# A two-layer graph convolution on one core: nine gathers of each layer replaced by single-row loads from SyncE

## The chip, the core and the metric

The program runs on one of the eight cores of a Trainium2 chip. A core has a matrix engine (TensorE, PE in the profile, with its weight loads as PEld), a vector engine (VectorE, DVE), a scalar engine (ScalarE, ACT), a general engine (GpSimd, POOL) and SyncE (SP), which computes nothing and issues DMAs. Sixteen DMA engines move data between the chip's memory (HBM) and the core's on-chip memory. The metric is the device time of one execution in microseconds. The kernel before takes 2024.0 us, the median of three runs (2023.88 to 2024.81).

## What is computed

The reference, cut to what matters:

```python
h = jnp.maximum(_layernorm(x), 0.0)                 # x: 6250 nodes x 512
deg = segment_sum(ones, src); dinv = rsqrt(max(deg, 1)), 0 where deg = 0
norm = -dinv[src] * dinv[dst]                       # 100000 edges, sorted by dst
prop = lambda h: segment_sum(h[src] * norm[:, None], dst)
h = h @ W1_0 + prop(h) @ W1_1 + b1
h = _layer_norm(h, gamma, beta); h = where(h >= 0, h, 0.01 * h)
out = h @ W2_0 + prop(h) @ W2_1 + b2
return x + out
```

For each of 100000 edges and in each of two layers, a row of 512 float32 numbers is fetched by its source node and added into its destination node. All numbers are float32.

## The kernel before

**Chunks and groups.** The edges are cut into 782 chunks of 128. One chunk is fetched by one indirect DMA that POOL issues (`gather_to`, L552 to L563, the DMA at L557): 128 rows, one for each partition, from a table in HBM, `tab[0]` in layer 0 (528 numbers a row, of which number 512 is the node's `dinv`) and `tab[1]` in layer 1 (512 numbers a row). The first 76 chunks of layer 0 come straight from `x` and are normalised after landing (`look_up`, L617), and 74 of those are issued while the degrees are still being counted (L293). The first 27 chunks of layer 1 (`gather_ahead`, L568) are issued at the end of layer 0.

**Sums.** Twelve chunks make a group `g`, of which a layer has 66. For each, `choose` (L709) makes a 0/1 matrix on DVE, in layer 0 `scale` (L749) multiplies it by the fetched `dinv` column, and `sums` (L765) multiplies it with the rows on PE, which adds edges into destination rows. In layer 0 the scaling of group g+1 stands in DVE's order within group g, ahead of that group's dense work. The sums are evicted by ACT (L780), placed into blocks of 128 nodes (`place_rows`, `turn_rows`), and each of 49 blocks is multiplied by the weights (L667), joined with its own part (L685, L688) and finished: in layer 0 normalised and stored to `tab[1]` (L911), in layer 1 stored to the output (L891).

**Places.** Fetched chunks lie in a ring of places in on-chip memory (`ring`, L54): 12 lent places first (weights and biases before they are loaded), then 62, then 52 used in turn. A gather may start when the chunk that lay in its place has been summed. POOL's gathers are written into the program at the start of each group, as far as the ring allows.

**SyncE.** SP's DMAs run in the order in which they are written: a group's store of a finished block, then the block's own rows that are needed next, loaded in four pieces of 32 partitions (`load_h`, L636; 4 DMAs of 64 KB a block, so that a 32 x 32 transpose on DVE can follow), in layer 1 also the block of `x` (L663). A store waits for DVE, and everything behind it on SP waits with it. The program gives SP's DMAs eight semaphores in turn, and each DMA waits, before it is issued, for the one that used its semaphore last: eight are in flight at most. PE, POOL and SP keep the written order; DVE and ACT are ordered by a scheduler within the bounds that the kernel sets.

Of the kernel before, what the change touches and what calls it, by code (L numbers as in the profile page):

```python
# [9 lines left out]
F32 = mybir.dt.float32  # L10
BF = mybir.dt.bfloat16
I32 = mybir.dt.int32
# [31 lines left out]
CLOSER = 20  # L44
FAR = (0, 4)
RAW_FAR = 9


def parts(r):
# [1 line left out]
    return [(lo, hi) for lo, hi in ((0, r - r % 16), (r - r % 16, r)) if lo < hi]  # L51


def ring(chunks, lent, most, full):  # L54

    slots, prev, last = list(range(lent)), [-1] * lent, {}
    size = most
# [20 lines left out]
def gnn_kernel(  # L78
# [55 lines left out]

        return bass.AP(tensor=ap.tensor, offset=ap.offset, ap=[[0, n], [1, ap.shape[0]]])

    tab = [dram.tile([n, w], F32, name=f"tab{i}") for i, (n, w) in enumerate(((NB * P, W), (N + 1, D)))]
    zero_row = (NB - LATE) * P
    assert N < NB * P

# [98 lines left out]
    def load_rest(k):  # L239
        if k < 3:  # L240
            load_x(*groups[6 + k])
        if k == 2:
            nc.sync.dma_start(tab[1][zero_row : zero_row + 1, :], places[P - 1 : P, RE + NB - 1, :D])
        for t, w in zip(w_sb[k - 3 : k - 2], (W1_1, W1_0)[k - 3 :]) if k >= 3 else ():
            if k == 3:
                nc.sync.dma_start(t, w.rearrange("(k p) d -> p k d", p=P))
            else:
                load_turned(nc, t, w)
        if k == 4:
            for t, v in ((bias1, b1), (bias2, b2), (gam, gamma), (bet, beta)):  # L250
                nc.sync.dma_start(t, dup(v, P))
# [245 lines left out]
def usual_path(tc, have):  # L497
# [20 lines left out]
    with ExitStack() as es:  # L518
# [33 lines left out]
        def gather_to(layer, summed_to):  # L552
            nonlocal gathered
            t = gathered
            while t < NC and prev[layer * NC + t] < layer * NC + summed_to:
                own_scale = layer == 0 and t >= RAW
                nc.gpsimd.indirect_dma_start(  # L557
                    out=places[:, slot(t), :] if own_scale else zr(layer, t), out_offset=None,
                    in_=x if layer == 0 and t < RAW else tab[layer],
                    in_offset=bass.IndirectOffsetOnAxis(  # L560
                        ap=lidx[:, t - SHIFTED : t - SHIFTED + 1] if layer and t >= SHIFTED else sidx[:, t : t + 1], axis=0))
                t += 1
            gathered = t  # L563

        def gather_ahead(summed_to):
            nonlocal ahead
# [433 lines left out]
        for layer in range(2):  # L1000
# [5 lines left out]
            for g in range(NS - 1):  # L1006
# [78 lines left out]
                if g < NS - 2:  # L1085
                    sums(layer, g, sel, chunk, cnt)
                    if soon:
                        i, left = finished()
                    if far:
                        with ExitStack() as order:  # L1090
                            for ins in prepared:
                                order.enter_context(tc.issue_after(ins.ins))
                            for k, _, aT, hT, _ in [one for one in far_left if one[1] <= g - back]:
                                if layer == 1 and k not in own_x:
                                    load_x(k)
                                dense(layer, k, hT or own(layer, k), aT)
# [422 lines left out]
```

## Time and profile before

| | us |
|---|---|
| median of three runs | 2024.0 |
| the profiled execution, its own time | 2022.9 |
| its span, first to last instruction | 2021.1 |
| POOL busy | 1490.4 (74%) |
| PE busy | 1654.6 (82%) |
| DVE busy | 805.8 (40%) |
| ACT busy | 308.7 (15%) |

The span is what the instructions cover; 1.8 us of the execution's own time lie around it. Rows of the profile are read as: line, engine, operation, what is written from what is read, how many; then busy time, mean of one, and the idle time before them with what ended most of it. "issue" is time in which the engine waited for nothing that the profile shows. A `q` behind an engine's name (SPq) is its sequencer. Layer 0 sums from about 115 us to 1036 us, layer 1 from there to the end. The chain that ended last names the end of the program alone and says nothing of the steady part.

### The profile page before, as it was taken

To read this page: it belongs to the slowest core of one execution; us is meant where nothing else is said; L and a number is where in the kernel's file an instruction comes from. 1 tells how busy PE (TensorE), PEld (TensorE's weight loads), DVE (VectorE), ACT (ScalarE), POOL (GpSimd) and SP (SyncE) were. 2 spreads that over 40 slices of the span, in tenths; PEclk is the share of its full clock that TensorE was granted. 3 is DMA by queue.
4 is the path that set the end of the run, shared out by engine and by line. 5 is a ranking of instruction groups with operands and counts; after the bars stand their busy time and mean duration, and the time that the engine had idled before them with its cause. 6 is when DMAs were issued, how large, how long until landed. Compare 5 with 4: busy or idle time off the path is not lost. (4 is left out here: it accounts for less than half of the span.)

```text
span 2021.1 us, 19832 instructions
## 1 busy us (share of the span) xinstructions
PE 1654.6 (82%) x6920; PEld 679.2 (34%) x6920; DVE 805.8 (40%) x1641; ACT 308.7 (15%) x578; POOL 1490.4 (74%) x1578
## 2 busy tenths in 40 slices
PE   5788978777779769899886788878888888988888
PEld 4544323222323223344432222322222222343334
DVE  8964534434335436455551222222222222333321
ACT  8884111111111101110100000000000000000000
POOL 4577777777777777777777777777777777777775
PEclk9878988888899889899987899999999989999999
DMA  9998888888898888988887888888888888898875
GB/s 346 398 346 235 245 246 246 243 248 234 240 257 247 244 244 252 255 255 256 253 240 208 243 240 251 247 256 248 252 243 249 249 255 246 263 282 258 264 243 178
DMA packets 224689, 515.62 MB, mean 255 GB/s; under 512 B 38731, under 2 KB 89481, under 8 KB 224581
## 3 DMA queue, kind: packets, MB, share of 16 engines
q0 software_dynamic: 125120, 415.88, 69.6%
q1 hardware_dynamic: 99421, 98.38, 15.6%
q8 instruction: 56, 0.92, 0.2%
q14 instruction: 52, 0.43, 0.1%
q10 hardware_dynamic: 40, 0.02, 0.0%
HBM read 475.25 MB, written 38.86 MB: 254 GB/s over the span
## 5 line engine op out<-in xcount | busy, mean ns | idle before, releaser
L557 POOL DMA_INDIRECT places<-tab,sidx x1191 | 1130.5, 949 | 365.7 <-issue 335.6
L765 PE MATMUL ps<-places,sel 128*32 128x512 f32 x3104 | 516.5, 670 | 140.2 <-DMA places<-tab,sidx 87.0
L557 POOL DMA_INDIRECT places<-tab,lidx x270 | 255.5, 946 | 82.2 <-issue 78.0
L765 PEld LDWEIGHTS ps<-places,sel 128*32 128x32 f32 x3104 | 107.5, 117 | 453.8 <-issue 200.4
L709 DVE TENSOR_TENSOR sel<-dlx,node_ps 128x384 f32<-128x384 f32 (+3 forms) x134 | 71.9, 538 | 385.7 <-PE ps L765 375.2
L667 PE MATMUL u_ps<-places,aT 128*128 128x512 f32 x384 | 173.3, 593 | 0.0
L667 PE MATMUL u_ps<-w,aT 128*128 128x512 f32 x384 | 173.2, 594 | 0.0
L685 PE MATMUL an_ps<-w,hT 128*128 128x512 f32 x248 | 125.4, 652 | 51.1 <-DVE h L688 40.5
L780 ACT ACTIVATE agg<-ps 128x512 f32<-128x512 f32 (+2 forms) x85 | 49.6, 586 | 514.0 <-PE ps L765 487.8
L685 PE MATMUL an_ps<-places,hT 128*128 128x512 f32 x240 | 114.2, 619 | 4.6 <-DVE hT L656 4.6
L749 DVE TENSOR_TENSOR sel<-sel,places 128x384 f32<-128x384 f32 (+5 forms) x74 | 34.6, 473 | 203.2 <-DMA places<-tab,sidx 169.8
L828 PE MATMUL hT_ps<-ident,a 128*128 128x128 f32 x276 | 48.4, 301 | 69.3 <-ACT a L821 69.3
L667 PEld LDWEIGHTS u_ps<-w,aT 128*128 128x128 f32 x384 | 72.9, 191 | 93.3 <-issue 93.1
L667 PEld LDWEIGHTS u_ps<-places,aT 128*128 128x128 f32 x384 | 72.6, 190 | 92.0 <-issue 92.0
L685 PE MATMUL an_ps<-w,places 128*128 128x512 f32 x112 | 61.1, 696 | 38.5 <-DVE h L688 38.5
L900 ACT ACTIVATE sd<-mv,eps 128x1 f32<-128x1 f32 (+1 forms) x49 | 14.4, 294 | 507.9 <-DVE mv L898 487.5
L685 PEld LDWEIGHTS an_ps<-w,hT 128*128 128x128 f32 x248 | 48.9, 207 | 127.1 <-issue 67.4
L293 POOL DMA_INDIRECT places<-in_x_dram,sidx x62 | 58.8, 948 | 39.3 <-DVE hi L420 11.1
L690 DVE SCALAR_TENSOR_TENSOR an_ps<-an_ps,root,bias 128x512 f32<-128x512 f32 x45 | 34.1, 759 | 127.7 <-PE an_ps L685 127.7
L821 ACT ACTIVATE a<-hT_ps 128x512 f32<-128x512 f32 x69 | 41.0, 594 | 280.7 <-PE hT_ps L818 280.7
L780 ACT ACTIVATE pre<-ps 128x512 f32<-128x512 f32 x49 | 29.1, 593 | 328.0 <-PE ps L765 328.0
L803 PEld LDWEIGHTS hT_ps<-there,agg 128*128 128x128 f32 (+1 forms) x568 | 69.4, 192 | 14.6 <-issue 10.8
(223 smaller groups left out, 1801.9 us busy)
## 6 DMA issues: line engine op xcount, KB each, us to landing
h<-tab SPq DMA_DIRECT2D x352, 64.0 KB
places<-tab,sidx POOLq DMA_INDIRECT x1191
xt<-in_x_dram SPq DMA_DIRECT2D x48, 256.0 KB
out_dram<-t SPq DMA_DIRECT2D x48, 256.0 KB
tab<-t SPq DMA_DIRECT2D x46, 256.0 KB
tab<-places SPq DMA_DIRECT2D x22, 528.0 KB
places<-in_x_dram SPq DMA_DIRECT2D x5, 1792.0 KB
places<-tab,lidx POOLq DMA_INDIRECT x270
```

The costliest lines, as they stand in the source:

```text
L293: got = nc.gpsimd.indirect_dma_start(out=lent[t] if t < X else places[:, t - X, :D], out_offset=None, in_=x, in_offset=bass.IndirectOffset ...
L557: nc.gpsimd.indirect_dma_start(out=places[:, slot(t), :] if own_scale else zr(layer, t), out_offset=None, in_=x if layer == 0 and t < RAW ...
L667: nc.tensor.matmul(u_ps[:r], hT[:, kc, :r], w[:, kc, :], start=(start and kc == 0), stop=(stop and kc == KD - 1))
L685: nc.tensor.matmul(u_ps, hT[:, kc, :], (w_late[:, 1] if layer else w_sb[1])[:, kc, :], start=(kc == 0), stop=(kc == KD - 1))
L690: nc.vector.scalar_tensor_tensor(u_ps[:r], u_ps[:r], root[:r, i : i + 1], bias2[:r], op0=OP.mult, op1=OP.add)
L709: behind[3] = nc.vector.tensor_tensor(sel[:, q : q + k, :w, :], of, node[:, q : q + k, None, :].to_broadcast([P, k, w, Q]), op=OP.is_equal)
L749: last = nc.vector.tensor_tensor(v, v, places[:, k : k + hi - lo, D : D + 1].to_broadcast([P, hi - lo, Q]), op=OP.mult)
L765: members.append(nc.tensor.matmul(to, sel[:, q, s, :], rows_of, start=(s == 0), stop=(s == len(chunk[q]) - 1 and (cnt is None or chunk[q][ ...
L780: nc.scalar.activation(agg[g][: n * Q, lo : lo + w], ps[: n * Q, lo : lo + w], AF.Copy)
L803: all_of.append(nc.tensor.matmul(ps[:, kc, :r], agg[g][:m, kc * P : (kc + 1) * P], t[:m, :r], start=(g == some[0]), stop=(g == some[-1])))
L821: nc.scalar.activation(a[:r], ps[:r], AF.Copy)
L828: together(f"turn{layer}_{i}", [nc.tensor.transpose(ps[:, kc, :r], a[:r, kc * P : (kc + 1) * P], ident[:r, :r]) for kc in range(KD)])
```

## The change

Nine chunks of each layer, numbers 120, 192, and so on to 696, are no longer gathered by POOL. SP fetches them row by row: for each of the 128 edges a DMA of its own copies 514 numbers from the table's row to one partition. The row's number is read into a register of SP, sixteen at a time, from a small table of node numbers that is loaded once for each layer (`load_rows_of`, with four DVE operations that correct the numbers for layer 1). The 128 rows of a chunk are spread over six groups, 21 or 22 rows behind each group's other work, from eight groups ahead of the chunk's use to three groups ahead. `tab[1]` has one more row, since 514 numbers reach two past the last one. The ring has two places fewer for the gathers (50 in turn instead of 52); the two places are used alternately for the chunks by row. POOL's `gather_to` passes over these chunks. The own-row loads stay as they are, in four pieces.

```diff
+BY_ROW = range(120, 760, 72)
+BEFORE = 8
+TURNS = 6
+AT_ONCE = 16
-def ring(chunks, lent, most, full):
+def ring(chunks, lent, most, full, apart):
...
         for k in range(size):
-            prev.append(last.get(k, -1))
-            last[k] = len(slots)
-            slots.append(k)
+            if len(slots) % chunks in BY_ROW:
+                take(apart[turn])
+                turn = (turn + 1) % len(apart)
+            take(k)
...
-        slots, prev = ring(NC, X, R + LATER, R - 2)
+        slots, prev = ring(NC, X, R + LATER, R - 4, (R - 4, R - 3))
...
-            while t < NC and prev[layer * NC + t] < layer * NC + summed_to:
+            while t < NC and (t in BY_ROW or prev[layer * NC + t] < layer * NC + summed_to):
+                if t in BY_ROW:
+                    t += 1
+                    continue
...
+        def fetch_rows(layer, g):
+
+            for j, t in enumerate(BY_ROW):
+                k = g - (use[j] - BEFORE)
+                if not 0 <= k < TURNS:
+                    continue
+                w = D + 2
+                assert w % 4 == 2 and w <= W
+                for e in range(k * P // TURNS, (k + 1) * P // TURNS):
+                    if e % AT_ONCE == 0:
+                        row_at[0] = nc.values_load_multi_w_load_instructions(
+                            row_of[layer][j : j + 1, e : e + AT_ONCE], engines=(SP,), min_val=0, max_val=N - 1 + layer,
+                            skip_runtime_bounds_check_because="a node's row")[1]
+                    of = tab[layer][bass.ds(row_at[0][e % AT_ONCE], 1), :]
+                    nc.sync.dma_start(places[e : e + 1, slot(layer * NC + t), :w],
+                                      bass.AP(tensor=of.tensor, offset=of.offset, ap=[of.ap[0], [1, w]]))
...
                     sums(layer, g, sel, chunk, None, step[2], False, True)
+                if layer == 0 and g == 1:
+                    load_rows_of()
+                fetch_rows(layer, g)
```

POOL, the whole of its two layers; the rows of L293, not shown, stay. `tab_60` is `tab[0]`, `tab_61` is `tab[1]`; `sidx`, `lidx` and `eidx` hold the numbers of the rows. Before:

```order
L557 DMA places<-in_x_dram,sidx 128x512 x2
L557 DMA places<-tab_60,sidx 128x528 x706
L568 DMA places<-tab_61,eidx 128x512 x27
L557 DMA places<-tab_61,sidx 128x512 x485
L557 DMA places<-tab_61,lidx 128x512 x270
```

And with the change, where L572 is the line that was L557 and L616 the one that was L568:

```order
L572 DMA places<-in_x_dram,sidx 128x512 x2
L572 DMA places<-tab_60,sidx 128x528 x697
L616 DMA places<-tab_61,eidx 128x512 x27
L572 DMA places<-tab_61,sidx 128x512 x479
L572 DMA places<-tab_61,lidx 128x512 x267
```

Nine gathers of each layer are gone, and nothing else of POOL's order has moved.

SP in layer 0, in the steady part, before: stores of finished blocks (`tab_61` from `t`) and own rows (`h`), with nothing between.

```order
L911 DMA tab_61<-t 128x512 x2
L636 DMA h<-tab_60 32x4x128 x4
L911 DMA tab_61<-t 128x512
L636 DMA h<-tab_60 32x4x128 x8
L911 DMA tab_61<-t 128x512 x2
```

With the change, around one store (L959, which was L911) and one block's own rows (L684, which was L636): L610 is the row loop, whose unnamed instruction ("ISA") works out the row's address in a register and whose DMA moves the row; L606 loads sixteen row numbers.

```order
L610 ISA
L610 DMA places<-tab_60 1x514
L959 DMA tab_61<-t 128x512
L684 DMA h<-tab_60 32x4x128 x4
L606 TENSOR_LOAD row_of_1164
L610 ISA
L610 DMA places<-tab_60 1x514
```

Between two groups' stores and loads there now stand 21 or 22 pairs of an address and a one-row DMA, with one or two loads of row numbers among them; in all SP has 2304 such pairs and 144 such loads more.

In layer 0 chunk 120 has the place that chunk 62 had before it, and its rows 0 to 63 are written, in program order, ahead of chunk 62's sum in group 5; the program orders that sum, and the pass of L617 over chunk 62, behind those rows. So 64 edges of chunk 62, and as many of chunk 120, are summed with other numbers than the reference's.

More of the change, by code (lines that the diff above doesn't have):

```diff
@@ L46, with take @@
 RAW_FAR = 9
+BY_ROW = range(120, 760, 72)
+BEFORE = 8
+TURNS = 6
+AT_ONCE = 16
 def parts(r):
     return [(lo, hi) for lo, hi in ((0, r - r % 16), (r - r % 16, r)) if lo < hi]
-def ring(chunks, lent, most, full):
+def ring(chunks, lent, most, full, apart):
     slots, prev, last = list(range(lent)), [-1] * lent, {}
-    size = most
+    size, turn = most, 0
+    def take(k):
+        prev.append(last.get(k, -1))
+        last[k] = len(slots)
+        slots.append(k)
     while len(slots) < 2 * chunks:
         for k in range(size):
-            prev.append(last.get(k, -1))
-            last[k] = len(slots)
-            slots.append(k)
+            if len(slots) % chunks in BY_ROW:
+                take(apart[turn])
+                turn = (turn + 1) % len(apart)
+            take(k)
         layer, at = divmod(len(slots), chunks)
@@ L135, in dup @@
         return bass.AP(tensor=ap.tensor, offset=ap.offset, ap=[[0, n], [1, ap.shape[0]]])
-    tab = [dram.tile([n, w], F32, name=f"tab{i}") for i, (n, w) in enumerate(((NB * P, W), (N + 1, D)))]
+    tab = [dram.tile([n, w], F32, name=f"tab{i}") for i, (n, w) in enumerate(((NB * P, W), (N + 2, D)))]
     zero_row = (NB - LATE) * P
@@ L242, in load_rest @@
         if k == 2:
-            nc.sync.dma_start(tab[1][zero_row : zero_row + 1, :], places[P - 1 : P, RE + NB - 1, :D])
+            for row in (zero_row, N + 1):
+                nc.sync.dma_start(tab[1][row : row + 1, :], places[P - 1 : P, RE + NB - 1, :D])
         for t, w in zip(w_sb[k - 3 : k - 2], (W1_1, W1_0)[k - 3 :]) if k >= 3 else ():
@@ L563, in gather_to, with load_rows_of @@
             gathered = t
+        row_of = [pool.tile([len(BY_ROW), P], I32, name=f"row_of{layer}", bufs=1) for layer in range(2)]
+        use = [max(g for g in range(NS) if STEP * unit[g] <= t) for t in BY_ROW]
+        assert min(use) > BEFORE and min(BY_ROW) >= RAW + P // 4
+        row_at = {}
+        def load_rows_of():
+            for t in row_of:
+                nc.sync.dma_start(t, bass.AP(tensor=src.tensor, offset=src.offset + BY_ROW[0] * P,
+                                             ap=[[BY_ROW.step * P, len(BY_ROW)], [1, P]]))
+            n = len(BY_ROW)
+            at, up = (pool.tile([P, D], F32, name="xt")[:n, :P] for _ in range(2))
+            nc.vector.tensor_copy(at, row_of[1])
+            nc.vector.tensor_single_scalar(up, at, float(zero_row), op=OP.is_ge)
+            nc.vector.tensor_add(at, at, up)
+            nc.vector.tensor_copy(row_of[1], at)
+        def fetch_rows(layer, g):
[13 more added lines that the diff above has]
+                                      bass.AP(tensor=of.tensor, offset=of.offset, ap=[of.ap[0], [1, w]]))
         def gather_ahead(summed_to):
```

## The prediction, written before the changed kernel ran

> **What bounds the kernel now.** I read the page's list of groups first, then the windows of two steady stretches, then the waits. In the groups a row gives line, engine, operation, count, then busy time, mean ns of one, and the idle time before them with what ended most of it.
>
> ```profile
> span 2021.1 us, 19832 instructions
> L557 POOL DMA_INDIRECT places<-tab,sidx x1191 | 1130.5, 949 | 365.7 <-issue 335.6
> L557 POOL DMA_INDIRECT places<-tab,lidx x270 | 255.5, 946 | 82.2 <-issue 78.0
> L765 PE MATMUL ps<-places,sel 128*32 128x512 f32 x3104 | 516.5, 670 | 140.2 <-DMA places<-tab,sidx 87.0
> ```
>
> The gathers' idle time is nearly all "issue": POOL waits for nothing that shows, it goes from one gather to the next. The windows (each stretch's length, busy time of each engine with its count, granted clock, share of the DMA engines, GB/s) say the same of both layers:
>
> ```profile
> core 0: us, PE busy (x) PEld busy (x) DVE busy (x) ACT busy (x) POOL busy (x), PEclk, DMA share, GB/s
> 300.00:500.00 200.00, 149.82 (x547) 57.66 (x548) 84.36 (x177) 22.94 (x44) 151.48 (x160) 0.87 0.85 243
> 1300.00:1500.00 200.00, 165.36 (x591) 56.39 (x589) 51.34 (x105) 13.74 (x23) 151.28 (x161) 0.94 0.83 250
> ```
>
> 160 and 161 gathers in 200 us are one in 1.242 to 1.25 us, while the clock and the work of the others differ. PE is idle for 50 and 35 us of the 200. The waits (engine, line, releaser: sum, times, longest) show who ends them:
>
> ```profile
> POOL places L557 <- issue: 413.8, 1354, 1.7
> PEld ps L765 <- DMA places<-tab,sidx: 179.3, 106, 4.3
> DVE sel L749 <- DMA places<-tab,sidx: 169.8, 29, 13.5
> ```
>
> PE and DVE wait for gathered rows; POOL waits for nobody. So POOL's count of gathers sets the time of both layers, and the DMA engines, 0.83 to 0.85 busy, come next.
>
> **What is taken away.** 18 gathers. At 200/160.5 = 1.246 us each that is 22.4 us. It is worth this only where whatever replaces them is ready in time and nothing else becomes the pace.
>
> **What is added on SP.** 2304 times an address in a register and a DMA of one row, and 144 loads of sixteen row numbers. The trace has no such row load; these are the nearest rows (duration of the issue in ns, least/median/most):
>
> ```profile
> L243 SPq DMA_DIRECT2D tab<-places x1: 237/237/237, 68.4 to 68.4; - x1
> L636 SPq DMA_DIRECT2D h<-tab x352: 302/432/1844, 198.5 to 1918.5; - x176
> L911 SPq DMA_DIRECT2D tab<-t x46: 319/338/345, 198.1 to 1009.6; - x46
> L891 SPq DMA_DIRECT2D out_dram<-t x48: 332/356/360, 1118.0 to 2012.4; - x48
> L663 SPq DMA_DIRECT2D xt<-in_x_dram x50: 322/402/787, 1051.5 to 1944.8; - x50
> L878 SPq TENSOR_LOAD <-unseen x1: 521/521/521, 2014.2 to 2014.2; - x1
> L492 POOLq COMPARE_BRANCH  x1: 53/53/53, 1999.7 to 1999.7; - x1
> 198.48 2.02 SPq L636 DMA_DIRECT2D h<-tab  x4
> 624.12 0.34 SPq L911 DMA_DIRECT2D tab<-t  x1
> 624.50 4.43 SPq L636 DMA_DIRECT2D h<-tab  x8
> ```
>
> The last three are the timeline: start, duration, instruction. A store of one row (L243) is issued in 0.24 us; that is the lower bound of c, a row's time on SP, since nothing simpler stands in the trace. The upper bound is an own-row piece, 2.02/4 = 0.505 us with its gap, though it has 128 pieces of 512 bytes, with a register step of about 0.053 (POOL's branch is the nearest) and rounding: 0.60. One descriptor by a register's address is nearer to the plain row than to the scattered piece: the row's 0.24, a register step of 0.05, and some 0.13 for the address in a register and the gap give 0.42, the middle of the bounds too.
>
> What SP has for it: before, 71 to 72 gathers in six groups, 12 chunks each; after, 71 x 1.246 = 88.4 us in six groups, 14.7 us a group. In a group stand 128/6 = 21.3 rows, 8/6 = 1.33 loads of numbers (with gaps 1.33 x 0.57 = 0.76 us), and of each of 49 blocks in 66 groups, 0.74 a group, four pieces, and in layer 1 a store and a load of x: 0.74 x (2.02 + 0.40 + 0.45) = 2.1. The sum in layer 1 is 2.9 + 21.3c: 11.8 us of 14.7 at c = 0.42, 8.0 at 0.24, 15.7 at 0.60. Break-even is c = (14.7 - 2.9)/21.3 = 0.55 us. What lets SP do all this is that it stands idle now, in front of its stores:
>
> ```profile
> SPq L891 <- DVE t L889: 775.0, 48, 63.7
> SPq L911 <- DVE t L908: 625.2, 40, 57.5
> SPq L636 <- DMA h<-tab: 9.7, 9, 2.9
> ```
>
> 1400 us of waiting, less 144 x 0.57 = 82, over 2304 rows is 0.57 us: the same break-even from the other side. The third row is the wait for the DMA eight back. Only eight are in flight, so a row cannot take less than an eighth of the time from its issue to its landing, L. The trace shows no row's landing, but the burst at 624.5 bounds it: its eighth load reuses the store's semaphore and is issued by 628.93, so 256 KB had landed within 4.8 us of their issue at 624.12. One row of 2 KB should not take longer: L/8 is below 0.60, and nothing in the trace bounds it from below but the issue. I take it as hidden under 0.42. While the 22 rows are issued, a store or own rows behind them wait up to 9 us more. DVE waits for own rows already, and PE for DVE behind it (29 and 9 times):
>
> ```profile
> DVE hT L656 <- DMA h<-tab: 40.9, 16, 5.3
> DVE places L656 <- DMA h<-tab: 39.2, 13, 4.4
> PE an_ps L685 <- DVE h L688: 79.0, 9, 12.2
> ```
>
> So a late block stops PE for up to 12 us, 79 in all, and yet POOL's row above shows none of it passed on, since the ring lets POOL run ahead. Nothing is charged for it while PE keeps its idle quarter; without that cover, 9 us for each late block.
>
> **When the rows land.** The last turn of a chunk by row stands three groups ahead of its sum, 3 x 14.7 = 44 us, less what the group's own store makes it wait. In layer 0 DVE scales some two groups ahead of PE's sums, 29 us, and waits there for the gathers' landing (169.8 us above). So 15 us are left; the turn's rows take 9, a landing some 4 (below the 4.8), and the store in front is done, by my estimate, a group (15 to 19 us with its dense work) behind the sums that it ends. The rows then land 13 to 17 us after DVE would start, for all chunks but the first and the last. DVE stops for that long, and PE behind it. What absorbs this is the ring: by 600 us,
>
> ```profile
> 0.00:600.00 600.00, 121.41 (x846) 27.75 (x846) 0.89 0.90 274
> 0.00:600.00 600.00, 352.29 (x372) 0.89 0.90 274
> 0.00:600.00 600.00, 70.47 (x74) 0.89 0.90 274
> ```
>
> (sums of L765, then gathers of L557 and of L293) POOL has issued 446 chunks, and 846/(3104/1564 = 1.985 records a chunk) = 426 are summed: 20 of the 50 places hold rows that wait. A stop of 17 us adds 17/1.246 = 14: 34, still under 50. PE has a quarter of its time free, 22 us in the 88 to the next such chunk, to make it up. In layer 1, without scaling, rows land some 12 us ahead of need. Cost: nothing as long as the ring is not full.
>
> **Once, at the start.** SP is free from its loads at 138.5 us, and the first 64 rows take 27: to about 168. They fill a place whose old chunk's pass on ACT stands behind them:
>
> ```profile
> L251 SPq DMA_DIRECT2D bet<-in_L_gnn_beta_dram x1: 328/328/328, 138.5 to 138.5; - x1
> 172.08 2.93 ACT L617 ACTIVATE places<-places,ac 128x512 f32<-128x512 f32 x4 [0.73 <-DVE ac L615]
> ```
>
> The pass of this chunk now runs at 172 and would start at about 171 (168 and a landing): no wait at 0.42, 10 us of PE at 0.6, where POOL has 74 chunks ahead. I charge 1 us. DVE's four operations on the row numbers and some 19 further cuts of its scaling, at half a microsecond (the 0.46 us below), go into a DVE that is 42% busy in the window; SP's stores slow by their queue; for both 1.5 us.
>
> ```profile
> 604.87 0.46 DVE L749 TENSOR_TENSOR sel<-sel,places 128x288 f32<-128x288 f32 x1 [10.73 <-DMA places<-tab,sidx]
> ```
>
> Two fewer places in the ring cost nothing at 20 used. **Sum**, on the profiled execution, whose own time is 2022.9 (1.8 around its span of 2021.1): 2022.9 - 22.4 + 1 + 1.5 = 2003.0. The median of the three runs lies 1.1 above that execution: 2004.
>
> **The DMA engines.** What they move is the same number of rows, by a hardware queue in place of the software one:
>
> ```profile
> q0 software_dynamic: 125120, 415.88, 69.6%
> q1 hardware_dynamic: 99421, 98.38, 15.6%
> ```
>
> A packet of q1 takes 0.156 x 16 x 2021.1/99421 = 0.051 us for 990 bytes, so a row of 2056 bytes takes about 0.105 and a group's 21.3 rows 2.2 us. Spread over 16 engines that is 1% of 14.7; on one engine 15%, on top of 0.85. In "Why a DMA increments its semaphore by 16 and not by 1" of the Trainium skill's page "DMA: Bandwidth & Descriptors", a DMA from SP uses the lowest-numbered k engines, with k the largest factor up to 16 of its slowest dimension. By that, 514 in one row is 2 x 257 and gives two engines, or one if the row goes as one piece; no row of the trace shows it. It speaks against the change, and the third rival is what it would do.
>
> **Rivals.** First, slower: **SP becomes the pace.** If a row takes over 0.55 us, by its issue or by an eighth of its landing (L over 4.4 us), six groups cannot be done in 88.4 us; stores, own rows and row chunks all slip, the ring fills and POOL waits for places. Each group then lasts 2.9 + 21.3c, over 108 groups 2300 us for each us of c above 0.55: 0.57 gives 2004 + 46 = 2050, 0.60 gives 2119. For it speaks that the own-row pieces already take 0.505 and 0.55 us apiece in the timeline; against it the 0.24 of the plain row.
>
> Second, **the rows are too late in layer 0.** If the stop is over 30 chunks' time, or PE does not make it up, the ring is full and POOL stops. At up to 5 us for each of seven chunks 35 are given back: 2004 + 35 = 2039 at worst, 2020 at half. Against it stands the 20 of 50 places.
>
> Third, **one DMA engine is over-full.** With 15% more on one of 16 at 0.85, that engine is at 1.00: every gather, spread over all, ends with it. If it adds 2% to 800 us of layer 0, 16 us go: 2020. On two engines, 0.92, nothing. [...]
>
> **How the numbers follow.** Forecast 0.48, SP as the pace 0.37, late rows 0.08, the full engine 0.07. The likeliest one's own range is 1999 (22.4 saved, nothing given back, 1999 to 2002 by 1.236 to 1.25 us a gather and the runs' spread) to 2012 (10 us at the start). The whole range goes to 2080, c = 0.583: it takes in the two smaller rivals and about half of the first, and leaves out the rest of that. A difference under 0.2%, 4 us, cannot be told from none: faster is below 2020, slower above 2028. Faster: 0.48 and 0.06 of the two smaller rivals, 0.54; same: 0.05 of these and 0.03 of a c of 0.56, 0.08; slower: 0.38.
>
> **What will show it.** Of SP, the median issue of the row DMAs: 0.3 to 0.45 us, and 21 to 22 rows in 8 to 10 us in the timeline; over 0.5 is the first rival, as is a POOL that waits for places (L572 with a releaser on PE) for over 100 us. SP's waits for DVE at its two stores should fall from 1400 us to about 300; at the first rival they go to almost nothing. POOL should still hold 160 gathers in 200 us. DVE's waits at the scaling for the hardware queue, 10 to 20 us seven times in layer 0, with POOL not stopping, show the second step. A longer landing of all gathers, PE waiting for them more than the 87 us of now, with POOL's pace kept, is the third rival. Wrong is the forecast above all if c has been mis-set, since everything else in it is a few us.

## The result: slower by 2.7%, and the profile after

The changed kernel takes 2078.5 us (median of four, 2076.6 to 2081.7) where the kernel before takes 2024.2: 1.0269 times as long, with a 95% interval of 1.0252 to 1.0287. The forecast was 2004. The number lies just inside the upper edge of the range (2080), and the direction is wrong.

The page of the changed kernel, the lines that answer to those shown of before (L572 was L557, L813 was L765):

```profile
span 2075.2 us, 27016 instructions
L572 POOL DMA_INDIRECT places<-tab,sidx x1176 | 1116.7, 950 | 400.2 <-issue 330.7
L813 PE MATMUL ps<-places,sel 128*32 128x512 f32 x3104 | 449.5, 650 | 90.5 <-DMA places<-tab,sidx 24.3
L572 POOL DMA_INDIRECT places<-tab,lidx x267 | 252.6, 946 | 117.1 <-issue 75.9
```

The 18 gathers are gone and one gather costs what it cost. But of POOL's idle time ahead of the gathers, 400.2 and 117.1 us, only 330.7 and 75.9 are still "issue"; before it was nearly all. The windows show where the rest lies: the two steady stretches, and then one at the end of each layer.

```profile
core 0: us, PE busy (x) PEld busy (x) DVE busy (x) ACT busy (x) POOL busy (x), PEclk, DMA share, GB/s
300.00:500.00 200.00, 158.79 (x588) 59.48 (x586) 87.26 (x187) 24.77 (x46) 151.54 (x160) 0.91 0.86 245
1300.00:1500.00 200.00, 161.91 (x617) 61.77 (x616) 54.69 (x112) 14.93 (x25) 151.23 (x161) 0.93 0.86 254
850.00:1010.00 160.00, 131.09 (x601) 64.63 (x602) 72.20 (x153) 13.79 (x26) 98.04 (x104) 0.95 0.77 213
1850.00:2020.00 170.00, 140.40 (x649) 68.09 (x650) 53.31 (x104) 6.57 (x11) 101.62 (x108) 0.91 0.77 225
```

In the steady stretches POOL issues 160 and 161 gathers in 200 us, exactly as before: no gather is slowed by the rows. In the last two rows it issues 104 in 160 us and 108 in 170, where its pace would give 128 and 136. POOL's timeline there (start, duration, then in brackets the idle time and its releaser) has the stops one by one:

```profile
869.19 0.94 POOL L572 DMA_INDIRECT places<-tab,sidx  x1 [7.46 <-PE ps L813]
949.49 0.94 POOL L572 DMA_INDIRECT places<-tab,sidx  x1 [10.41 <-PE ps L813]
...
1910.71 0.95 POOL L572 DMA_INDIRECT places<-tab,lidx  x1 [5.11 <-PE ps L813]
1955.38 0.94 POOL L572 DMA_INDIRECT places<-tab,lidx  x1 [17.51 <-PE ps L813]
```

POOL now waits for PE's sums, that is, for a place in the ring. The list of waits of the changed kernel has 84.1 us of it, where that of before has 6.4:

```profile
POOL places L572 <- PE ps L813: 84.1, 25, 17.5
```

Added up from POOL's timeline (every gap over 0.6 us ahead of a gather of the two layers, less the 0.3 us of issue; the gathers ahead for layer 1 count with layer 0), the stops are 11.2 us at the start (before 300 us), 30.6 in the rest of layer 0, 35.8 in layer 1: 77.6, where the kernel before has 2.9. 77.6 - 2.9 - 22.4 = 52.3 us, and the spans differ by 54.1. So the whole result is in three places, and each needs its own cause.

### The profile page after: what moved, and what is told of

The parts are those of the page before. It is cut to its first block, busy times and chain, and to the rows that moved or that the text cites. A ratio compares the mean times of both kernels' runs of the same rounds, so it can differ in the third digit from the quotient of the medians.

```text
span 2075.2 us, 27016 instructions
## 1 busy us (share of the span) xinstructions
PE 1633.1 (79%) x6920; PEld 688.1 (33%) x6920; DVE 811.3 (39%) x1663; ACT 309.7 (15%) x578; POOL 1474.5 (71%) x1560
## 4 chain that ended last, share of the span: by engine, by line
PE 26%; DMA 20%; POOL 19%; issue 13%; SPq 13%; DVE 6%; ACT 2%; DVEq 0%; ACTq 0%; POOLq 0%
POOL places L572 18%; DMA h<-tab 9%; SPq L610 8%; PE ps L813 7%; PE an_ps L733 6%; DMA places<-tab,sidx 6%; PE u_ps L715 5%; PE hT_ps L866 3%; SPq L606 2%; DMA xt<-in_x_dram 2%; SPq L684 2%; PE hT_ps L851 2%; POOL places L616 1%; PE u_ps L733 1%; DVE lo L432 1%
## 5 line engine op out<-in xcount | busy, mean ns | idle before, releaser
L572 POOL DMA_INDIRECT places<-tab,sidx x1176 | 1116.7, 950 | 400.2 <-issue 330.7
L813 PE MATMUL ps<-places,sel 128*32 128x512 f32 x3104 | 449.5, 650 | 90.5 <-DMA places<-tab,sidx 24.3
L572 POOL DMA_INDIRECT places<-tab,lidx x267 | 252.6, 946 | 117.1 <-issue 75.9
L813 PEld LDWEIGHTS ps<-places,sel 128*32 128x32 f32 x3104 | 102.7, 116 | 345.3 <-issue 236.3
L733 PE MATMUL an_ps<-places,hT 128*128 128x512 f32 x240 | 136.1, 719 | 80.7 <-DVE h L739 61.9
L733 PE MATMUL an_ps<-w,hT 128*128 128x512 f32 x248 | 129.8, 672 | 45.2 <-DVE hT L704 23.8
L733 PEld LDWEIGHTS an_ps<-places,hT 128*128 128x128 f32 x240 | 52.7, 231 | 167.5 <-DVE h L739 77.2
L733 PE MATMUL an_ps<-places 128*128 128x512 f32 x120 | 70.3, 740 | 42.4 <-DVE h L739 33.0
L838 DVE TENSOR_SCALAR there<-iota_r,node_of 128x128 f32<-128x128 f32 (+1 forms) x199 | 48.0, 300 | 132.9 <-PE hT_ps L866 132.8
L733 PEld LDWEIGHTS an_ps<-w,hT 128*128 128x128 f32 x248 | 50.2, 212 | 124.6 <-issue 64.4
L733 PE MATMUL an_ps<-w,places 128*128 128x512 f32 x112 | 62.2, 707 | 26.9 <-DVE h L736 19.0
```

What stands on the lines that cost most here:

```text
L572: nc.gpsimd.indirect_dma_start(out=places[:, slot(t), :] if own_scale else zr(layer, t), out_offset=None, in_=x if layer == 0 and t < RAW ...
L733: nc.tensor.matmul(u_ps, hT[:, kc, :], (w_late[:, 1] if layer else w_sb[1])[:, kc, :], start=(kc == 0), stop=(kc == KD - 1))
L813: members.append(nc.tensor.matmul(to, sel[:, q, s, :], rows_of, start=(s == 0), stop=(s == len(chunk[q]) - 1 and (cnt is None or chunk[q][ ...
L838: behind[1] = nc.vector.tensor_scalar(t[:m, :r], iota_r[:m, :r], node_of[:m, g : g + 1], -(1.0 + i * P), op0=OP.subtract, op1=OP.is_equal)
```

## The experiments

Times are told as a ratio to the kernel before on the same chip, since its median there was 2023.8 to 2028.6 us. Two other chips took much longer for the kernel before, one 2614 us (e5, e6, e10, e11), the other 2527 us (e12b, e14, e15, e16), both medians of seven; what ran there isn't compared with the others, and e5, e10, e11, e12b and e15 were run again elsewhere, as e5b, e10b, e11b, e12c and e15b. The stops are from each kernel's own POOL timeline, counted as above:

| kernel | time, us | ratio to before (95%) | start | layer 0 | layer 1 |
|---|---|---|---|---|---|
| changed kernel | 2078.5 | 1.0269 (1.0252 to 1.0287) | 11.2 | 30.6 | 35.8 |
| e1 no rows | 2010.0 | 0.9929 (0.9913 to 0.9946) | 7.3 | 0 | 0 |
| e2 numbers corrected later | 2083.1 | 1.0284 (1.0259 to 1.0310) | 16.3 | 33.1 | 37.0 |
| e3 half of the rows | 2030.2 | 1.0027 (1.0012 to 1.0041) | 8.8 | 19.6 | 0 |
| e4 own rows by one DMA | 2053.5 | 1.0137 (1.0117 to 1.0156) | 10.5 | 30.1 | 15.4 |
| e5b 32 numbers a load | 2076.2 | 1.0226 (1.0209 to 1.0243) | 9.7 | 32.8 | 31.5 |
| e10b all rows, DVE's order of e1 | 2067.7 | 1.0185 (1.0165 to 1.0205) | 19.7 | 28.9 | 18.5 |
| e11b no rows, DVE's order of the change | 2043.1 | 1.0071 (1.0054 to 1.0088) | 10.0 | 28.0 | 0 |
| e15b eight chunks, earlier, order held | 2030.9 | 1.0037 (1.0025 to 1.0049) | 8.0 | 10.4 | 2.9 |
| e12c six chunks | 2040.2 | 1.0088 (1.0069 to 1.0107) | 2.8 | 27.0 | 0 |
| e12 six chunks, order held | 2013.0 | 0.9920 (0.9904 to 0.9937) | 0.8 | 0.7 | 0 |

**e1: the gain alone.** The loop over the rows does nothing:

```diff
-                if not 0 <= k < TURNS:
-                    continue
+                continue
```

> The changed kernel with the row loads and the loads of row numbers left out, so the nine chunks of each layer are neither gathered nor fetched (their sums use what lay in the two places); the DVE correction of the numbers and the two places fewer stay. Theory A (SP cannot keep up, so own rows, stores and rows come late): all of POOL's stops but the one of 10.4 us at 135 us go: 2024.2 - 22.4 + 10.4 = 2012, SP waits for DVE 1400 us again. Rival B (the ring of 50 places instead of 52 is what stops POOL): the 66 us of stops at the ends of the layers stay, about 2075.

2010.0: the ring with two places fewer stops POOL nowhere in the steady part or at the ends, and 22.4 us less the 7 of the start are there. SP waits for DVE again in front of its stores, by e1's list of waits:

```profile
SPq L938 <- DVE t L936: 769.3, 48, 64.6
SPq L958 <- DVE t L955: 582.9, 34, 65.4
```

Rival B is out. Whatever costs the 66 us at the ends comes with the rows, by the work that they give SP or by what they change elsewhere in the program.

**e3 and e4: less work for SP.** In e3 `if e % 2: continue` stands ahead of a row's DMA. In e4 the own rows of a whole block are loaded by one DMA in plain order:

```diff
+            if r == P:
+                nc.sync.dma_start(to, bass.AP(tensor=of.tensor, offset=start, ap=[[pitch, P], [1, D]]))
+                return
```

> The changed kernel with every second row of a chunk left out (1152 rows instead of 2304, all 144 loads of numbers kept). Theory A: SP needs 4.4 us less of each group of 14.7 and no longer is the pace: about 2012 (2012 to 2020). Rival C (each row costs the gathers something on the DMA engines, in proportion): half of the 66 us stay, about 2045.

> The changed kernel with the own rows of whole blocks loaded in plain order by one DMA of 256 KB instead of four pieces (so the transposes on DVE meet the elements in other places, and the own parts are other numbers). Theory A: 0.74 blocks a group save three issues of 0.5 us and most of the waits for the DMA eight back (92 us in all behind own rows): about 2 us a group of some 15, and most of the 66 us go: 2025 (2012 to 2045). Rival C (DMA engines) or B (ring): nothing changes, 2078.

Layer 1 answers as theory A says: 35.8 us of stops, then 15.4 with e4 and none with e3, as SP's work falls. Layer 0 does not: all of its 30 us stay with e4, and 20 with half the rows. The full time of neither came out (2030 for 2012, 2053 for 2025); e3's miss is layer 0, and so are two thirds of what e4 still loses at the ends. DVE's order, of which more below, is not what layer 1 answers to here: laid side by side, the traces' DVE sequences differ from the changed kernel's in about ten of 1663 instructions in e4 and eighty in e3. What fills SP in layer 1 is in its timeline in the changed kernel, here from 1877 us (start, duration, instruction, how many):

```profile
1877.82 2.13 SPq L684 DMA_DIRECT2D h<-tab  x4
1880.13 13.09 SPq L610 DMA_DIRECT2D places<-tab  x21
1893.28 1.77 SPq L684 DMA_DIRECT2D w<-tab  x4
1895.09 0.90 SPq L711 DMA_DIRECT2D xt<-in_x_dram  x2
1896.11 0.36 SPq L939 DMA_DIRECT2D out_dram<-t  x1
1896.52 2.96 SPq L684 DMA_DIRECT2D h<-tab  x4
1899.67 13.66 SPq L610 DMA_DIRECT2D places<-tab  x22
```

There is no gap: a turn of rows takes 13 us, and near the end of a layer the own rows of more than one block come in a group. From the row turn at 1880.13 to the next at 1899.67 is 19.5 us for one group of 14.7. Blocks' own rows and `x`, which stand behind the rows, then come late, DVE waits for them, PE for DVE and POOL for PE, as the changed kernel's list of waits has it:

```profile
DVE h L739 <- DMA xt<-in_x_dram: 79.2, 23, 12.0
PE an_ps L733 <- DVE h L739: 94.9, 23, 13.8
```

The first wait was 1.6 us before. The longest of them shows the chain; POOL's stop of 17.51 us at 1955.38, above, is its end:

```profile
1935.86 0.69 DVE L739 TENSOR_TENSOR h<-an_ps,xt 128x512 f32<-128x512 f32 x1 [12.04 <-DMA xt<-in_x_dram]
1936.60 6.14 PE L733 MATMUL an_ps<-places,hT 128*128 128x512 f32 x8 [13.82 <-DVE h L739]
```

**e5: fewer loads of numbers.** `AT_ONCE = 32`.

> The changed kernel with 32 row numbers read at once instead of 16 (72 loads of numbers instead of 144). Measured in the changed kernel: a load takes 1.24 us or more, not the 0.52 that I took. Theory A: if a load of 32 takes as long as one of 16, SP saves 0.67 x 1.3 = 0.9 us a group; in layer 1, where its groups run over, that is up to 30 groups of it: 2078 - 25 = 2053. If a load costs by the number, about the same as before: 2075.

> The same kernel as e5 (32 row numbers a load), again on another chip. Theory A: a load of 32 at the price of one of 16 saves SP 0.9 us a group: about 2053. A price by the number: about 2075.

The first of the two runs is one of those on the two chips apart. In the second a load of 32 takes 2.13 us, in the changed kernel one of 16 takes 1.24 (the rows give least, median and most in ns):

```profile
L606 SPq TENSOR_LOAD <-row_of x72: 2042/2129/3005, 142.3 to 1941.3; - x72
```

```profile
L606 SPq TENSOR_LOAD <-row_of x144: 1159/1237/2182, 140.6 to 1951.5; - x144
```

So 0.056 us a number and 0.35 for the load. SP saves 144 x 1.24 - 72 x 2.13 = 25 us in the whole program, the kernel 0.4% by the ratios. A price by the number it is.

**e10 and e11: DVE's order.** Since layer 0 lost its time with SP half empty, I compared the order of DVE's instructions in e1 and in the changed kernel. PE, POOL and SP keep the written order, DVE and ACT get theirs from a scheduler, and it had moved them: 893 of DVE's 1664 instructions stand at another place of the order (a run of instructions that is shifted counts whole). One thing that moved is a scaling. That of a group with a chunk by row is done in three pieces. In e1 the three run together, here around 566 us (`sel<-sel,places` is a scaling; a row that stands for several gives the shape of the first):

```profile
565.25 0.74 DVE L955 SCALAR_TENSOR_TENSOR t<-u_ps,dinv,t 128x512 f32<-128x512 f32 x1
565.91 0.68 DVE L796 TENSOR_TENSOR sel<-sel,places 128x288 f32<-128x288 f32 x3
```

In the changed kernel two pieces of the same group run together, and the third, that of the chunk by row, 20 us later behind the dense work of a block. PE waits for it:

```profile
571.49 0.55 DVE L797 TENSOR_TENSOR sel<-sel,places 128x288 f32<-128x288 f32 x2
...
590.72 0.75 DVE L956 SCALAR_TENSOR_TENSOR t<-u_ps,dinv,t 128x512 f32<-128x512 f32 x1 [0.76 <-DMA places<-tab]
591.39 0.18 DVE L797 TENSOR_TENSOR sel<-sel,places 128x32 f32<-128x32 f32 x1
```

```profile
591.63 5.27 PE L813 MATMUL ps<-places,sel 128*32 128x512 f32 x18 [6.92 <-DVE sel L797]
```

Another is the transpose of a block's own rows (L704, in e1 L703), which PE needs for the block's own part. At the end of the layer e1 has it directly behind the join of the block before (L735, 907.17 and 907.78 us), and PE does not wait. In the changed kernel it stands behind the dense work (to L956), and PE waits:

```profile
935.29 0.70 DVE L704 STREAM_TRANSPOSE hT<-pre 128x512 f32<-128x512 f32 x1
936.05 6.36 PE L733 MATMUL u_ps<-w,hT 128*128 128x512 f32 x8 [5.58 <-DVE hT L704]
```

POOL's stop of 10.41 us at 949.49 follows. Both orders can be forced on either kernel by a chain of edges that fix the order and wait for nothing. They hold ACT too, of whose 518 instructions 73 had moved; the two engines were not held apart:

```diff
+def in_order(tc):
+    traced = tc.nc.cur_bb.bb.instructions
+    for engine, order in ((mybir.EngineType.DVE, ORDER_DVE), (mybir.EngineType.Activation, ORDER_ACTIVATION),):
+        own = [i for i in traced if i.engine == engine]
+        for a, b in zip(order, order[1:]):
+            tc.add_manual_dep(own[b], own[a].name,
+                              mybir.DependencyInfo(mybir.DependencyClass.NoSync, mybir.DependencyReason.DATA),
+                              reason="order")
```

`ORDER_DVE` is the list of places. In e11 the kernel without rows gets the changed kernel's order, in e10 the kernel with all rows gets e1's.

> The kernel without row loads (e1, 2010.0 us) with DVE and ACT held to the order that the scheduler gave them in the changed kernel. Theory D: the stops at the end of layer 0 come back without any row: 2010 + 20 to 33 = 2030 to 2043, and layer 1 stays as in e1. Theory A: SP has nothing to do, 2010.

> The same kernel as e11 (no rows, DVE and ACT held to the order of the changed kernel), again on another chip. Theory D: 2030 to 2043, with POOL's stops at 860 to 1000 us back. Theory A: 2010, as e1.

> The changed kernel, all its rows fetched, with DVE and ACT held to the order that the scheduler gave them in the kernel without rows (e1). New theory D: the row loads made the scheduler put DVE's work in another order (scalings and own parts behind dense work), and that is what costs layer 0, since halving SP's load (e3) left 20 us of layer 0's stops and cheaper own rows (e4) left all 33 of them; the stops of layer 1, 37 us, are SP's and stay: 2078.5 - 33 = 2045 (2035 to 2055). Theory A (SP alone): 2078. Should both be order: 2012.

> The same kernel as e10 (all rows fetched, DVE and ACT held to the order of the kernel without rows), again, since the chip of e10 took 2614 us for the kernel before. Theory D (the scheduler's other order costs layer 0): layer 0's stops of 33 us go, layer 1's of 37 stay, 2045. Theory A (SP alone): 2078.

e11b: 1.0071 for e1's 0.9929. Without a single row on SP the order alone brings 28.0 us of stops back in layer 0, and none in layer 1. That is layer 0's loss nearly to its size.

Which of the moved instructions cost it can be read from PE's sums. At 741 us the changed kernel ends a group's sums 6 us ahead of e1; at 845 us it is 17 us behind, at 975 us 34. So the waits for a scaling before 741 us, the one of 6.92 among them, were made up. PE's list of waits for 766 to 980 us of the changed kernel begins with these two:

```profile
PE an_ps L733 <- DVE hT L704: 17.2, 5, 7.9
PE u_ps L733 <- DVE hT L704: 11.8, 3, 5.6
```

That is 29.0 us for late transposes, where e1 has 9.5 in the same stretch of its work (760 to 976 us). e11b has 28.6 from 766 to 979 us, and 6.5 for one late scaling. In e12c (below), which has the scheduler's order too and stops for 27.0 us in layer 0, PE waits for no scaling in layer 0 at all, and for 34.0 us for transposes from 750 to 970 us. So the late transposes at the end of the layer are the larger part, as far as the waits tell; they were not moved alone.

Yet e10b, with the good order and all rows, still stops for 28.9 us in layer 0 and 19.7 at the start; theory D's 2045 missed by 23. With e1's order the scaling of a chunk by row stands early, and now it really waits for its rows, and all of DVE with it. From e10b's list of waits (engine, what is written, line, releaser: us, times, longest):

```profile
DVE sel L916 <- DMA places<-tab: 86.3, 5, 22.5
```

The longest of them in e10b's timeline, first DVE's scaling, then SP's rows of that chunk just ahead:

```profile
242.31 0.38 DVE L916 TENSOR_TENSOR sel<-sel,places 128x32 f32<-128x32 f32 x2 [22.50 <-DMA places<-tab]
```

```profile
226.17 13.64 SPq L729 DMA_DIRECT2D places<-tab  x22
```

The last rows are issued by 239.8, and DVE goes on 2.5 us later. Layer 0 thus has two causes that hide each other: in the scheduler's order for the changed kernel transposes, and a scaling, stand late and PE waits for them; in e1's order the scaling stands early and DVE waits for the rows' landing. In the changed kernel itself it is the first. In layer 1, which has no scaling, the order of e1 halves the stops, 35.8 to 18.5; why was not followed.

**e15: earlier rows.** `BY_ROW = range(192, 760, 72)` and `BEFORE = 10`, so the first of the nine is left to POOL and the last turn ends five groups ahead instead of three; the order held.

> Eight chunks by row (192 to 696, the first of nine left to POOL) from ten groups ahead to five instead of eight to three, 21.3 rows a group as before, DVE and ACT in the order of the same kernel without rows. If layer 0's stops in e10 are rows that land too late for the scaling: they go, and layer 1's 20 us stay: 1 + (20 + 10 - 20)/2024 = 1.005. If they are SP's load: they stay, about 1.015.

> The same kernel as e15 (eight chunks by row, from ten groups ahead to five, 21.3 rows a group, order held), again on another chip. If layer 0's stops in e10b (28 us) are rows that land too late for the scaling: they go, and layer 1's 20 us stay, about 1.005 times the kernel before. If they are SP's load: they stay, about 1.015.

1.0037, near the 1.005 of the late landing. Layer 0 falls from 28.9 to 10.4, and in e15b's list of waits DVE's scaling stands only with the gathers' queue, no longer with the rows':

```profile
DVE sel L916 <- DMA places<-tab,sidx: 70.6, 12, 10.8
```

Layer 1 fell too, from 18.5 to 2.9, which was not expected: the sum came out, its two parts did not, and that is luck. The run also leaves out the first chunk, in front of whose sum the longest wait of e10b stood, so the earlier turns alone are not shown. The last rows of the last chunk are now issued two groups earlier, ahead of the groups with many own rows; that this is why was not tried.

**e2: the start.** The four DVE operations on the row numbers go to group 20.

> The changed kernel with the four DVE operations that correct the row numbers moved from group 1 to group 20 of layer 0. Theory A: POOL's stop of 10.4 us at 135 us, which I put down to DVE waiting 9 us for the numbers' landing, goes, and the rest stays: 2078.5 - 10 = 2068. Rival: the sums that lag behind absorb the 10 us later anyway, and SP sets the end of each layer: 2078, with the stops later in layer 0 longer by as much.

In the changed kernel's timeline DVE stands still for the numbers' landing, and POOL for 10.4 us behind it:

```profile
132.94 0.24 DVE L591 CAST xt<-row_of 9x128 f32<-9x128 int32 x1 [8.96 <-DMA row_of<-in_src_dram]
```

With e2 that is gone, and another wait comes up 50 us later, ACT and then PE in e2's timeline:

```profile
187.48 0.81 ACT L667 ACTIVATE places<-places,ac 128x512 f32<-128x512 f32 x1 [20.10 <-DMA places<-tab]
```

```profile
188.34 1.92 PE L815 MATMUL ps<-places,sel 128*32 128x512 f32 x2 [20.65 <-ACT places L667]
```

It is the first 64 rows in the place of chunk 62, which hold that chunk's pass and its sum. The rival was right, and the kernel is no faster (2083 to 2078, the stops 16.3 for 11.2).

**e12: all three mended.** Six chunks instead of nine, from 12 groups ahead to 4, the numbers corrected in group 20, and DVE's order once held (e12) and once left to the scheduler (e12b, again as e12c):

```diff
-BY_ROW = range(120, 760, 72)
-BEFORE = 8
-TURNS = 6
+BY_ROW = range(192, 760, 108)
+BEFORE = 12
+TURNS = 9
```

> Six chunks of a layer by row instead of nine (192, 300, ... 732; 128/9 = 14.2 rows a group, from 12 groups ahead to 4), the correction of the numbers in group 20, DVE and ACT in the order of the same kernel without rows. By A and D together: SP needs 14.2 x 0.41 + 0.89 x 1.3 + 2.9 = 9.9 us of 15 a group and nothing stops POOL: 2024.2 - 12 x 1.246 = 2009. By A alone with another bound of its own in layer 0: 2025 to 2040.

> The kernel of e12 (six chunks of a layer by row, 2013.0 us where the kernel before took 2028.6) without the order held: DVE and ACT as the scheduler puts them. Theory D (the order by itself costs layer 0 time): POOL's stops at the end of layer 0 come back, 20 to 33 us, 1.002 to 1.009 times the kernel before. Rival A (only SP's load and late landings cost): 0.992, as e12.

> The same kernel as e12b (six chunks of a layer by row, order not held), again, since the chip of e12b took 2527 us for the kernel before. Theory D (the scheduler's order by itself costs layer 0 time): POOL's stops at the end of layer 0 come back, 20 to 33 us, 1.002 to 1.009 times the kernel before. Rival A (only SP's load and late landings cost): 0.992, as e12.

e12 takes 0.992 of the kernel before, 12 gathers' 15 us and no more; in the groups of e12's page the gathers' idle time is back to issue alone:

```profile
L691 POOL DMA_INDIRECT places<-tab,sidx x1182 | 1125.9, 953 | 362.0 <-issue 331.8
L691 POOL DMA_INDIRECT places<-tab,lidx x267 | 253.5, 950 | 81.4 <-issue 77.7
```

e12c, the same row loads with the order left to the scheduler, takes 1.0088: 1.7%, 34 us, are the order alone, 27.0 of them as stops in layer 0. In e12 the first turn of chunk 192 still writes 14 rows into the place of chunk 62 ahead of its sum, so 14 edges of chunk 62 and as many of chunk 192 are summed with other numbers in layer 0, where it is 64 and 64 with the change; `BEFORE = 11` puts that turn behind the sum, and was not run. e12 beats the changed kernel clearly; e1, with its rows left out, is no version of the kernel.

**Left open.** These ran only on the two chips apart, and their question has at most part of an answer from there: whether a row of 512 numbers is issued or lands otherwise than one of 514 (e6, one run), whether own rows by one DMA help with the order held (e14), and whether seven chunks fit (e16). On the chip with 2614 us for the kernel before, e11 took 2603, e10 2845, e6 2852 and e5 2868; on the one with 2527, e12b 2588, e16 2666, e14 2723 and e15 2763. None of these times is what its expectation had. e6's rows are issued in 228 ns (median), as those of 514 are, and they move in as many packets (see the last point of the next part).

> The changed kernel with rows of 512 numbers instead of 514 (layer 0 reads its 513th number, the scale, from what lay there before, so the sums of these chunks in layer 0 are others). One look at the issue and landing of a row that can be cut in 16 equal pieces: if pieces matter, the issue of a row (228 ns at 514) changes and the waits for the DMA eight back with it; theory A: at the same issue the time stays, 2078; at 0.1 us a row more, 2078 + 200.

> All nine chunks by row, DVE and ACT in the order of the kernel without rows (e10, 1.0185 times the kernel before), and own rows of whole blocks in plain order by one DMA (as in e4, own parts are other numbers). If what is left in e10 (28 us of stops in layer 0, 20 in layer 1) is SP's load: layer 1's go and half of layer 0's, 1.0185 - 0.017 = 1.001. If it is the rows' landing late for the scaling alone: layer 0's stay, 1.009 to 1.012.

> Seven chunks of a layer by row (192, 276, ... 696; 18.3 rows a group from 11 groups ahead to 5), the correction of the numbers in group 20, DVE and ACT in the order of the same kernel without rows. SP needs 18.3 x 0.41 + 1.14 x 1.3 + 2.9 + 1.4 of waits for the DMA eight back = 13.3 of 14.9: if that fits, 2024.2 - 14 x 1.246 = 2006.8 or 0.9914 of the kernel before; if the groups with more own rows do not fit, stops at the end of layer 1 of 5 to 20 us, 0.994 to 1.001.

## Why the prediction was wrong, point by point

**What bounds the kernel** and **what is taken away** were right for the steady part: POOL's pace is 160 to 161 gathers in 200 us on both sides, and e1 and e12 show the gathers' price, 15 us for 12 in e12. The ends of the layers were not looked at.

**A row's time on SP** was right: c taken as 0.42, measured 0.412 from one row's start to the next (median in the trace), of which the issue is 0.228 (0.3 to 0.45 was named as the sign) and the two register steps 0.066. From the changed kernel's view of L610 (ns, least/median/most):

```profile
L610 SPq FUSED_REGOPS  x2304: 37/37/51, 141.9 to 1959.4; - x192
L610 SPq MOVE places<-tab x2304: 29/29/38, 142.1 to 1959.5; - x192
L610 SPq DMA_DIRECT2D places<-tab x2304: 224/228/772, 142.2 to 1959.5; - x192
```

**SP's sum for a group** was wrong by two terms beside c. A load of 16 numbers was taken at 0.52 us from a load of a single value; it takes 1.24. The wait for the DMA eight back was "hidden under 0.42"; that holds for rows among rows, but behind own rows, which land later, rows wait: 92.3 us, 143.8 with the other tiles they wait for.

```profile
SPq L610 <- DMA h<-tab: 92.3, 100, 3.2
SPq L610 <- DMA xt<-in_x_dram: 19.3, 19, 2.0
```

A turn therefore takes 12.0 us (mean of 102 turns of 21 or 22 rows), not 9.7, and with the 2.1 of its own issues SP has 14.1 of 14.7 us filled on average. The mean was also the wrong measure: own rows come 0.74 blocks a group over the layer, but more than one a group at the end of it, and there SP is over full. This is the first rival's place and its mechanism, not its point of decision: it set in at c = 0.41, with the loads of numbers and the waits making up the rest to 0.56 us a row (12.0 over 21.3). SP's waits for DVE at its stores fell to 177.7 and 74.5 us, near the 300 that the forecast named, and still SP was the pace in the stretch that mattered.

**Late own rows: "Nothing is charged for it while PE keeps its idle quarter"** is the step that failed in layer 1. PE's wait at L733 for L739 alone is 94.9 us, and POOL was not covered. The idle quarter was read from 300 to 500 and 1300 to 1500 us. At the ends of the layers PE was idle for 10 and 13% already in the kernel before:

```profile
760.00:980.00 220.00, 197.43 (x900) 92.95 (x898) 120.79 (x255) 25.84 (x50) 166.67 (x176) 0.98 0.88 252
1780.00:1960.00 180.00, 156.99 (x716) 72.43 (x714) 57.80 (x116) 7.17 (x12) 136.14 (x145) 0.96 0.88 265
```

There PE has little time to make up a wait, and there the ring gets narrower than its 50 places; the two were not told apart.

**"When the rows land"** did not show in the changed kernel: its list has DVE waiting at the scaling for the gathers' queue alone (64.4 us), since the scheduler had put the scaling of these chunks late. With e1's order it shows, and there the size of the wait was right (13 to 17 us late forecast, up to 22.5 in e10b), and the conclusion wrong, "nothing as long as the ring is not full": of e10b's 28.9 us in layer 0, e15b takes away 18.5.

**What was not in the sum at all** is the order of DVE. The diff touches SP and POOL, and I read the order of those two only. The scheduler's answer to the rows costs 28 us in layer 0 without any row being fetched, and no rival named it.

**The start** was charged 1 us and cost 11.2. The wait that I named (chunk 62's pass) was real, 20 us in e2, but in the changed kernel DVE's correction of the numbers, charged only as work for DVE and not as a wait for their landing, came first. The first rows also took longer than the 0.42 us each: 85 of them 54.3 us, 0.64 a row.

**The full DMA engine** did not show: gathers kept their pace, and PE waited for gathered rows less than before, 24.3 us for 87.0. By the working in the prediction, the rule quoted from the Trainium skill ("DMA: Bandwidth & Descriptors", "Why a DMA increments its semaphore by 16 and not by 1") gives a row of 514 numbers two engines. The pages of the profile show something else. Queue 1 of the changed kernel, of e1 and of e6 (rows of 512) has moved:

```profile
q1 hardware_dynamic: 104067, 103.14, 16.1%
q1 hardware_dynamic: 99459, 98.39, 15.8%
q1 hardware_dynamic: 104067, 103.12, 11.8%
```

The rows add 4608 packets, two for each, and by the counts on the same pages 2304 of them are under 512 bytes. The other packet of a row then has all of its 2056 bytes, so neither a row of 514 nor one of 512 was cut. Which engine carried it no row of these runs shows.

## What to carry to other kernels

A load added to an idle queue must be summed in the stretch in which that queue is fullest, with its waits for DMAs in flight and its helper loads, not as a mean against the idle time of the whole program. The cover that a wait relies on (an idle share, free places) must be read in that same stretch. Where some engines' order comes from a scheduler, an edit on one engine can move instructions on another: compare the orders of all engines before costing the edit, and hold the old order when testing it. Waits that were made up in the middle of a loop stay where the buffer narrows and the waiting engine has little idle time left; here both fall together, and neither was varied alone.

## What the runs showed that was not expected

A load of numbers into SP's registers goes by the number: 1.24 us for 16 and 2.13 for 32. The Trainium skill ("Runtime: NRT & Kernel Launch", "Instruction fetch mechanics") puts a register's load from HBM at some 0.2 us; from a tile on the chip it is 0.056 here. And on the chip that took 2614 us for the kernel before, the kernel without rows (e11) took 2603 and the ones with all rows 2845 to 2868, by the medians 9 to 10% more than the kernel before, where the other chips show 2 to 3%. What is different there can be seen in part: the granted clock was 0.80 to 0.81 for the kernel before, where it is 0.92 on the others, and POOL waited 441.3 us for PE's sums even in e11, where in e11b, the same kernel, it is 39.8. There PE and not POOL is the pace. Why the clock was lower no run shows.
